# Softmax sums and value products of a window-attention unit on TensorE: issued one after the other, or side by side on alternating tiles

## The chip, the cores and the metric

The kernel runs on one core of one Trainium2 chip. The metric is the device time of one execution in microseconds (us), lower is better. All data are 32-bit floats.

## The reference

The input `x` is an image batch of shape 16 x 56 x 56 x 384 (batch, height, width, channels). Two layers follow each other, each with a residual connection:

```
x = x + attention(groupnorm(x))        # 7x7 windows, shifted by 3, 12 heads of 32
x = x + depthwise3x3(groupnorm(x))     # weights replaced by their signs
```

The attention of a window, per head, over its 49 tokens:

```
score = q @ k.T / sqrt(32) + bias      # 49 x 49, with masks in the last windows
attn  = softmax(score)                 # exp, divided by its sum over the keys
out   = attn @ v                       # 49 x 32
```

The change concerns the last two lines: the sums over the keys, by which the result is divided, and the products with the values.

## The kernel before, in words

**Strips and units.** An image is cut into 8 strips of 7 rows, a strip into 8 windows. The attention works on units of 4 windows, that is half a strip: there are 16 x 8 x 2 = 256 units, numbered `u`. An even `u` is the first half of a strip, an odd one the second.

**The scores come out transposed.** `scores` (line 570) leaves in PSUM, for each head, the keys on the partitions and the queries along the columns. Of the two windows of a pair, one has its keys on partitions 0 to 48, the other on 64 to 112. VectorE scales them and adds the bias (`softmax`, line 587), ScalarE takes the exponential (`exponential`, line 605). The result is the tile `es`, and it is not divided yet.

**Sums and products.** With the keys on partitions, TensorE can do both. `add_up` (line 640) multiplies a matrix of ones, 49 x 32, with the exponentials: each output row holds the sum over the keys, 32 times over, which is what the division needs. There are 8 such matmuls in a unit, one for each of four groups of heads (`i`) and two windows of a pair (`w`), with 294 columns each. `attend` (line 661) multiplies values, 49 x 32, with exponentials, 49 columns at a time: 48 matmuls a unit, over 3 heads of a group (`j`), 2 pairs (`r`), and again `i` and `w`.

**Tiles of TensorE.** Both kinds of matmul use 64 rows and 32 columns of the array at a time, and so one of 8 tiles: `w` chooses the upper or lower rows, `i` the columns. The order of the loops hands the tiles out in turn: `i` and `w` are the innermost loops. A 32-bit matmul of the program stands in the trace as two matmuls, each with a weight load of its own.

**What follows.** `invert` takes the reciprocal of the sums: a logarithm and an exponential on ScalarE (lines 679 and 680), then two operations on VectorE that refine it (lines 681 and 682). The sums lie in the PSUM banks that the scores had used, so the next unit's scores must wait until line 681 has read them. `attend` ends with two copies on ScalarE that bring the products from two PSUM banks (`po`) to SBUF (line 671). `divide` multiplies the two on VectorE (line 689). In an odd unit `project` (line 700) then multiplies the strip's result with the output weights.

**The order of the work.** It is written out by hand and no scheduler changes it. `all_units` goes over the units. Each has a list of six pieces of heavy work, `todo` (the matmuls with 128 x 128 weights and 392 columns: queries and keys at line 503, values at 516, the projection at 700). Sums, inversion, products and division come behind the first piece, the scores of the next unit behind the third (even units) or the fourth (odd units) piece. Between the pieces stands light work of the second layer (`side`), mostly on VectorE. The values reach `attend` through DMAs issued on SyncE's queue; `await_values` puts the wait for them on the first sum of a strip. Four PSUM banks are shared by all other matmuls in turn (`bank`).

Of the kernel before, what the change touches and what calls it, by code (L numbers as in the profile page):

```python
# [34 lines left out]
def kernel(  # L35
# [12 lines left out]
    nc = tc.nc  # L48
# [3 lines left out]
    D = C // NH  # L52
    NC = C // P
    HPC = P // D
    T = WIN * WIN
# [4 lines left out]
    UPS = NW // UW  # L60
    NU = NS * UPS
    HT = 64
# [30 lines left out]
    def bank(name):  # L93
        return ps.tile([P, 512], F32, tag="mm", name=name)
# [6 lines left out]
    ones = const.tile([P, P], F32, tag="ones", name="ones")  # L101
# [385 lines left out]
    raw, sums = {}, {}  # L487
# [12 lines left out]
    def query_key(s, m):  # L500
        pq = bank(f"pq_{s}_{m}")
        for c in range(NC):
            nc.tensor.matmul(  # L503
                pq[:, :ST].rearrange("p (w t) -> p w t", t=T),
                wq_t[:, c, m * P : (m + 1) * P],
                xn[:, c, :, :T],
                start=(c == 0),
                stop=(c == NC - 1),
            )
        nc.scalar.copy(qk[:, m, :ST], pq[:, :ST])  # L510

    def value(s, m):

        pv = bank(f"pv_{s}_{m}")
        for c in range(NC):
            nc.tensor.matmul(  # L516
                pv[:, :ST].rearrange("p (w t) -> p w t", t=T),
                wq_t[:, c, 2 * C + m * P : 2 * C + (m + 1) * P],
                xn[:, c, :, :T],
                start=(c == 0),  # L520
                stop=(c == NC - 1),
            )
        nc.scalar.copy(vt[:, m, :, :T], pv[:, :ST].rearrange("p (w t) -> p w t", t=T))  # L523

    def turn(s, m):

        nc.vector.transpose(  # L527
            vq[:, :, :, m].rearrange("p h n d -> p n h d"),
            vt[:, m].rearrange("p (n w) (j b) -> p n (w j) b", w=2, b=D),
        )  # L530
# [3 lines left out]
    def by_key(s):  # L534

        vs[s] = vpool.tile([P, HPC, NW // 2, NC, D], F32, tag="v", name=f"v_{s}")
        carried[s] = []
        for half in range(4):
            for i in range(HPC):
                move = nc.sync.dma_start(  # L540
                    vs[s][half * D : (half + 1) * D, i].rearrange("k n m d -> k (n m d)"),
                    vq[i * D : (i + 1) * D, half].rearrange("k n m d -> k (n m d)"),
                )
                carried[s].append(move.ins.name)

    def await_values(s, product):

        for name in carried.pop(s) if s else ():
            tc.add_manual_dep(
                product.ins,  # L550
                name,
                mybir.DependencyInfo(mybir.DependencyClass.Sync, mybir.DependencyReason.DATA),
                reason="values by key",
            )

    def scores(u, fast):


        s, n = divmod(u, UPS)
        pp = score_banks  # L560
        rows = T if fast else HT
        for j in range(NC):
            for r in range(2):
                for k in range(2 * HPC):
                    i, w = k % HPC, (k + k // HPC) % 2
                    part = slice(i * D, (i + 1) * D)
                    q0 = (n * UW + 2 * r + w) * T
                    row, col = (w, r) if fast else (r, w)
                    k0 = (2 * j + col) * T
                    nc.tensor.matmul(  # L570
                        pp[row * HT : row * HT + rows, i, k0 : k0 + T],
                        qk[part, NC * fast + j, q0 : q0 + rows],
                        qk[part, NC * (not fast) + j, q0 : q0 + T],
                        start=True,
                        stop=True,
                    )
        raw[u] = pp
# [50 lines left out]
    def by_head(u):  # L628

        flat = es.rearrange("k h w q -> k (h w q)")[:, : NH * 2 * T]  # L630
        return flat.rearrange("k (h r q) -> k h r q", h=NH, r=2)

    def add_up(u):

        flat = es.rearrange("k h w q -> k (h w q)")[:, : NH * 2 * T]
        su = raw[u][:, 0:2, : NC * 2 * T]
        for i in range(HPC):
            for w in range(2):
                keys = slice(w * HT, w * HT + T)
                product = nc.tensor.matmul(  # L640
                    su[i * D : (i + 1) * D, w],
                    ones[keys, :D],
                    flat[keys, i * NC * 2 * T : (i + 1) * NC * 2 * T],
                    start=True,
                    stop=True,
                )
                if u % UPS == 0 and i == 0 and w == 0:
                    await_values(u // UPS, product)
        sums[u] = su

    def attend(u, fast):
        s, n = divmod(u, UPS)
        if n == 0:
            ots[s] = two.tile([P, NC, ST], F32, tag="ot", name=f"ot_{s}")
        po = [bank(f"po_{u}_{w}") for w in range(2)]
        for j in range(NC):
            for r in range(2):
                for i in range(HPC):
                    for w in range(2):
                        keys = slice(w * HT, w * HT + T)  # L660
                        nc.tensor.matmul(  # L661
                            po[w][i * D : (i + 1) * D, (2 * j + r) * T : (2 * j + r + 1) * T],
                            vs[s][keys, i, n * 2 + r, j],
                            by_head(u)[keys, i * NC + j, r] if fast else pts[u, j][keys, 2 * i + r, :],
                            start=True,
                            stop=True,
                        )
        ot = ots[s][:, :, n * UW * T : (n + 1) * UW * T]
        by_window = ot.rearrange("p j (r w q) -> p j r w q", r=2, w=2)
        for w in range(2):  # L670
            nc.scalar.copy(
                by_window[:, :, :, w, :], po[w][:, : NC * 2 * T].rearrange("p (j r q) -> p j r q", j=NC, r=2)
            )

    def invert(u):

        su = sums[u]
        ln, inv = (ptpool.tile([P, 2, NC * 2 * T], F32, tag="pt", name=f"{name}_{u}") for name in ("ln", "inv"))
        nc.scalar.activation(ln, su, AF.Ln, bias=least)
        nc.scalar.activation(inv, ln, AF.Exp, scale=-1.0, accum_out=reach[:, 1, u : u + 1])  # L680
        nc.vector.scalar_tensor_tensor(ln, su, -1.0, inv, ALU.mult, ALU.mult)  # L681
        nc.vector.scalar_tensor_tensor(ln, ln, 2.0, inv, ALU.add, ALU.mult)  # L682
        sums[u] = ln
# [257 lines left out]
    side = {}  # L941
# [72 lines left out]
    def all_units(fast, meanwhile=None):  # L1014
        for m in range(NC):
            value(0, m)
            turn(0, m)
        by_key(0)
        for m in range(2 * NC):
            query_key(0, m)  # L1020
        if meanwhile:
            meanwhile()
        scores(0, fast)
        softmax(0, fast)
        normalize(1)
        exponential(0, fast)
        plan(nc.sync)
        for u in range(B * NU):
            todo = heavy(u)
            light = [(w, f, a) for w, f, a in sorted(side.pop(u, []), key=lambda i: i[0])]  # L1030
            more = u + 1 < B * NU

            then = NC if u % UPS else NC - 1
            for i in range(len(todo)):
                run(todo[i])
                if i == 0:
                    if fast:
                        add_up(u)
                    else:
                        for j in range(NC):  # L1040
                            transpose(u, j)
                    if fast:
                        invert(u)
                    attend(u, fast)
                    if fast:
                        divide(u)
                if i == then and more:
                    scores(u + 1, fast)
                    softmax(u + 1, fast)
                if i == then + 1 and more:  # L1050
                    exponential(u + 1, fast)
                while light and light[0][0] - u <= (i + 1) / len(todo):
                    _, g, a = light.pop(0)
                    g(*a)
            for _, g, a in light:
                g(*a)
        for _, g, a in sorted((i for u in side for i in side[u]), key=lambda i: i[0]):
            g(*a)
        side.clear()


    with tc.manual_schedule():
# [29 lines left out]
        def meanwhile():  # L1092
            load_weights(NC)
            add_bias(True)
            clear_conv()
# [80 lines left out]
```

## Time and profile before

| | us |
|---|---|
| median of 3 runs | 4033.58 (4032.53 to 4033.74) |
| profiled execution | 4033.27 |
| its span, first to last instruction | 4031.5 |
| TensorE busy with matmuls | 3951.1 (98%) |
| VectorE busy | 3493.7 (87%) |
| ScalarE busy | 2228.9 (55%) |
| GpSimd busy | 1871.3 (46%) |
| mean granted TensorE clock | 0.991 of full speed |

Busy time of TensorE is the time in which at least one matmul is under way. Matmuls overlap, above all those on different tiles, so a duration in the trace says how long one lasted, and not what it adds to the time; that is read from when the next ones begin. PEld is the weight loads, which run beside the matmuls. In a row of a line's source view, the three durations are minimum, median and maximum in ns. In the waits the three figures are us in total, the number of times, and the longest.

### The profile page before, as it was taken

Reading aid. Unit: us, or ns where it says so; the run is one execution under the profiler, and the core shown is the slowest. Engines: PE = TensorE matmul, PEld = TensorE weight load, DVE = VectorE, ACT = ScalarE, POOL = GpSimd, SP = SyncE. Lnnn points to the kernel's source line nnn. Section 1 sums busy time; section 2 is a strip of 40 time slices with the busy share of each in tenths; the row PEclk is TensorE's granted clock in tenths of the full one; section 3 lists DMA queues with packets and bytes.
Section 4 is the critical chain, followed back from the end, with each engine's and each line's share of the span. In section 5 each row is a group of like instructions: output and inputs, shape, how many; then the busy total and the mean of one; then the engine's idle time right before and its main releaser. Section 6 shows DMA issues by size and latency. Waiting matters only on the chain.

```text
span 4031.5 us, 144681 instructions
## 1 busy us (share of the span) xinstructions
PE 3951.1 (98%) x63189; PEld 2412.2 (60%) x63189; DVE 3493.7 (87%) x3718; ACT 2228.9 (55%) x4690; POOL 1871.3 (46%) x3168
## 2 busy tenths in 40 slices
PE   7999999999999999999999999999999999999987
PEld 5656555555556555556556556555655656556657
DVE  4546989899898998989899898998989899898897
ACT  3545556556565656556556564656556556565552
POOL 6554545355453554545355454554545455452000
PEclk8999999999999999999999999999999999999998
DMA  4323455554545554555554554554545554553444
GB/s 108 84 67 88 111 114 116 109 120 103 117 116 102 126 111 104 113 113 116 107 122 107 114 115 102 125 112 103 114 112 115 108 123 105 114 117 81 114 103 105
DMA packets 801364, 439.36 MB, mean 109 GB/s; under 512 B 671562, under 2 KB 750777, under 8 KB 800720
## 3 DMA queue, kind: packets, MB, share of 16 engines
q1 hardware_dynamic: 711110, 268.40, 31.1%
q0 software_dynamic: 88320, 161.19, 17.2%
q8 instruction: 498, 8.16, 0.9%
q14 instruction: 146, 1.20, 0.1%
q10 hardware_dynamic: 1290, 0.42, 0.0%
HBM read 170.08 MB, written 158.45 MB: 81 GB/s over the span
## 4 chain that ended last, share of the span: by engine, by line
PE 42%; issue 17%; DVE 15%; POOL 14%; DMA 8%; ACT 2%; SPq 1%; DVEq 0%; POOLq 0%; ACTq 0%
PE pq L503 16%; POOL xl L450 10%; PE pv L516 9%; PE py L700 8%; DVE o L828 6%; PE score_banks L570 3%; DMA xl<-in_x_dram 3%; PE po L661 3%; PE score_banks L640 2%; DVE e L587 2%; DVE xt L467 2%; DMA mvd<-mv 1%; DMA mid<-y 1%; DMA gt<-mvd 1%; DVE ln L682 1%
## 5 line engine op out<-in xcount | busy, mean ns | idle before, releaser
L503 PE MATMUL pq<-xn,wq_t 128*128 128x392 f32 x4608 | 1584.9, 496 | 0.0
L450 POOL DMA_DIRECT2D xl<-in_x_dram x1980 | 1331.8, 723 | 143.3 <-DVE xt L467 93.6
L828 DVE SCALAR_TENSOR_TENSOR o<-hp,dw_t,o 128x1568 f32<-128x1568 f32 x752 | 1378.2, 1833 | 5.4
L503 PEld LDWEIGHTS pq<-xn,wq_t 128*128 128x128 f32 x4608 | 845.4, 188 | 595.5 <-ACT x L482 0.4
L516 PE MATMUL pv<-xn,wq_t 128*128 128x392 f32 x2304 | 815.6, 497 | 13.5 <-DVE y L708 13.5
L700 PE MATMUL py<-ot,wo_t 128*128 128x392 f32 x2304 | 819.1, 501 | 7.4 <-DVE ot L689 6.3
L510 ACT COPY qk<-pq 128x392 f32<-128x392 f32 x768 | 368.4, 483 | 562.9 <-PE pq L503 562.7
L720 POOL COPY y<-y 128x63 f32<-128x63 f32 x128 | 56.5, 442 | 1205.2 <-DVE y L708 1205.1
L700 PEld LDWEIGHTS py<-ot,wo_t 128*128 128x128 f32 x2304 | 425.4, 190 | 312.0 <-DVE ot L689 26.0
L516 PEld LDWEIGHTS pv<-xn,wq_t 128*128 128x128 f32 x2304 | 424.4, 189 | 313.1 <-DVE y L708 15.6
L605 ACT ACTIVATE e<-e 128x1176 f32<-128x1176 f32 x256 | 303.2, 1184 | 500.5 <-DVE e L587 499.5
L681 DVE SCALAR_TENSOR_TENSOR ln<-score_banks,inv 128x588 f32<-128x588 f32 x256 | 195.9, 765 | 323.5 <-ACT inv L680 322.4
L523 ACT COPY vt<-pv 128x392 f32<-128x392 f32 x384 | 188.7, 492 | 359.2 <-PE pv L516 358.4
L570 PEld LDWEIGHTS score_banks<-qk 32*49 32x49 f32 x24576 | 266.4, 118 | 146.8 <-issue 115.8
L587 DVE SCALAR_TENSOR_TENSOR e<-score_banks,bias 128x1176 f32<-128x1176 f32 x256 | 347.1, 1356 | 6.1 <-PE score_banks L570 5.9
L661 PEld LDWEIGHTS po<-e,v 49*32 49x32 f32 x24576 | 311.0, 105 | 50.8 <-issue 0.8
L479 ACT COPY x<-xt 128x196 f32<-128x196 f32 x720 | 225.6, 368 | 176.9 <-DVE xt L467 176.7
L661 PE MATMUL po<-e,v 49*32 49x49 f32 x24576 | 309.7, 212 | 0.0
L570 PE MATMUL score_banks<-qk 32*49 32x49 f32 x24576 | 298.9, 218 | 4.4 <-DVE ln L681 2.9
L527 DVE STREAM_TRANSPOSE vq<-vt 128x512 f32<-128x512 f32 x384 | 265.6, 693 | 8.6 <-ACT vt L523 5.4
L492 ACT ACTIVATE xn<-x,coef 128x392 f32<-128x392 f32 x384 | 247.0, 711 | 6.4 <-DVE coef L381 6.4
L708 DVE TENSOR_TENSOR y<-py,x 128x392 f32<-128x392 f32 x384 | 213.2, 555 | 42.9 <-PE py L700 42.6
(183 smaller groups left out, 3303.7 us busy)
## 6 DMA issues: line engine op xcount, KB each, us to landing
v<-vq SPq DMA_DIRECT2D x2048, 48.0 KB
xb<-mid SPq DMA_DIRECT2D x90, 855.5 KB
out_dram<-o SPq DMA_DIRECT2D x736, 98.0 KB
mid<-y POOLq DMA_DIRECT2D x112, 619.5 KB
xl<-in_x_dram POOLq DMA_DIRECT2D x1260, 52.5 KB
mid<-y POOLq DMA_DIRECT2D x15, 354.0 KB
xl<-in_x_dram POOLq DMA_DIRECT2D x180, 28.0 KB
mid<-y POOLq DMA_DIRECT2D x15, 265.5 KB
```

Of the source, the lines that this page charges most:

```text
L450: nc.gpsimd.dma_start(xz[i * D + lo : i * D + hi, c, k : k + n, :], flat[token : token + n * (hi - lo)].rearrange("(k t) c -> t k c", k=n) ...
L492: nc.scalar.activation(xn[:, c, :, :T], xs[s][:, c, :].rearrange("p (w t) -> p w t", t=T), AF.Identity, bias=coef[:, c, 1:2], scale=coef[: ...
L503: nc.tensor.matmul(pq[:, :ST].rearrange("p (w t) -> p w t", t=T), wq_t[:, c, m * P : (m + 1) * P], xn[:, c, :, :T], start=(c == 0), stop=( ...
L510: nc.scalar.copy(qk[:, m, :ST], pq[:, :ST])
L516: nc.tensor.matmul(pv[:, :ST].rearrange("p (w t) -> p w t", t=T), wq_t[:, c, 2 * C + m * P : 2 * C + (m + 1) * P], xn[:, c, :, :T], start= ...
L527: nc.vector.transpose(vq[:, :, :, m].rearrange("p h n d -> p n h d"), vt[:, m].rearrange("p (n w) (j b) -> p n (w j) b", w=2, b=D),)
L570: nc.tensor.matmul(pp[row * HT : row * HT + rows, i, k0 : k0 + T], qk[part, NC * fast + j, q0 : q0 + rows], qk[part, NC * (not fast) + j, ...
L587: nc.vector.scalar_tensor_tensor(e, pp[:, :, : NC * 2 * T].rearrange("q i (n k) -> q i n k", k=T), QSCALE, bias[:, int(s % NS == NS - 1)]. ...
L605: nc.scalar.activation(flat, flat, AF.Exp, accum_out=reach[:, 0, u : u + 1])
L661: nc.tensor.matmul(po[w][i * D : (i + 1) * D, (2 * j + r) * T : (2 * j + r + 1) * T], vs[s][keys, i, n * 2 + r, j], by_head(u)[keys, i * N ...
L700: nc.tensor.matmul(py[:, :ST], wo_t[:, c, m * P : (m + 1) * P], ots[s][:, c, :], start=(c == 0), stop=(c == NC - 1),)
L828: nc.vector.scalar_tensor_tensor(acc, by_half(hp[:, dy : dy + BR, dx : dx + W]), dw_t[:, c, t : t + 1], acc, ALU.mult, ALU.add)
```

## The change

`add_up` takes a list of tiles and is called twice in a unit from within `attend`. The 8 tiles are split into two sides, those with an even and those with an odd `i + w`, as on a chessboard. First the four sums of one side are issued, then all 24 products of the other side, then the four sums of the other side, then the 24 products of the first. `invert` is issued behind all of these and ahead of the two copies; before, it was issued behind the sums and ahead of the products. On ScalarE the order of logarithm, exponential and copies stays as it was. The number and the sizes of the matmuls stay the same, and the wait for the values' DMAs stays on the first sum.

```diff
-    def add_up(u):
+    def add_up(u, tiles):
 
         flat = es.rearrange("k h w q -> k (h w q)")[:, : NH * 2 * T]
-        su = raw[u][:, 0:2, : NC * 2 * T]
-        for i in range(HPC):
-            for w in range(2):
-                keys = slice(w * HT, w * HT + T)
-                product = nc.tensor.matmul(
...
-                if u % UPS == 0 and i == 0 and w == 0:
-                    await_values(u // UPS, product)
-        sums[u] = su
+        first = u not in sums
+        su = sums.setdefault(u, raw[u][:, 0:2, : NC * 2 * T])
+        for i, w in tiles:
+            keys = slice(w * HT, w * HT + T)
+            product = nc.tensor.matmul(
+                su[i * D : (i + 1) * D, w],
+                ones[keys, :D],
+                flat[keys, i * NC * 2 * T : (i + 1) * NC * 2 * T],
+                start=True,
+                stop=True,
+            )
+            if first and u % UPS == 0:
+                await_values(u // UPS, product)
+            first = False
 
     def attend(u, fast):
...
-        for j in range(NC):
-            for r in range(2):
-                for i in range(HPC):
-                    for w in range(2):
+        tiles = [(i, w) for i in range(HPC) for w in range(2)]
+        sides = [[(i, w) for i, w in tiles if (i + w) % 2 == side] for side in range(2)]
+        for k in range(2):
+            if fast:
+                add_up(u, sides[k])
+            for j in range(NC):
+                for r in range(2):
+                    for i, w in sides[1 - k]:
                         keys = slice(w * HT, w * HT + T)
                         nc.tensor.matmul(
...
+        if fast:
+            invert(u)
         ot = ots[s][:, :, n * UW * T : (n + 1) * UW * T]
...
                 if i == 0:
-                    if fast:
-                        add_up(u)
-                    else:
+                    if not fast:
                         for j in range(NC):
                             transpose(u, j)
-                    if fast:
-                        invert(u)
                     attend(u, fast)
```

`fast` is true in the pass that runs here; the other is a fallback for sums out of range.

## The prediction

> **What bounds the kernel now.** I read the page's first part, then the sources of the two lines that move, then a timeline of one unit, and last that timeline cut at chosen instants, which counts the matmuls begun by then. Page and sources:
>
> ```profile
> PE 3951.1 (98%) x63189; PEld 2412.2 (60%) x63189; DVE 3493.7 (87%) x3718; ACT 2228.9 (55%) x4690; POOL 1871.3 (46%) x3168
> L640 PE MATMUL score_banks<-e,ones x4096: 407/432/696, 75.6 to 3926.1; 49*32 49x294 f32 x196
> L661 PE MATMUL po<-e,v x24576: 200/203/285, 76.6 to 3927.8; 49*32 49x49 f32 x200
> ```
>
> TensorE (PE) is occupied 98%, so what one unit costs it returns 256 times. A product in the program is two matmuls in the trace, a first and a second pass, each with its own weight load (PEld): a unit has 16 sum passes and 96 product passes. Timeline of one unit, PE alone (start, length, count):
>
> ```profile
> 2011.19 0.73 PE L640 MATMUL score_banks<-e,ones 49*32 49x294 f32 x16
> 2011.71 1.14 PE L661 MATMUL po<-e,v 49*32 49x49 f32 x96
> 2012.79 4.22 PE L516 MATMUL pv<-xn,wq_t 128*128 128x392 f32 x12
> ```
>
> Sums, products and hand-over take 2012.79 - 2011.19 = 1.60 us. The same stretch cut at 2011.46, 2011.47, 2011.72, 2011.76, 2011.82, 2011.89, 2011.905, 2012.66:
>
> ```profile
> 2011.19 0.48 PE L640 MATMUL score_banks<-e,ones 49*32 49x294 f32 x8
> 2011.19 0.68 PE L640 MATMUL score_banks<-e,ones 49*32 49x294 f32 x9
> 2011.71 0.21 PE L661 MATMUL po<-e,v 49*32 49x49 f32 x2
> 2011.71 0.25 PE L661 MATMUL po<-e,v 49*32 49x49 f32 x9
> 2011.71 0.29 PE L661 MATMUL po<-e,v 49*32 49x49 f32 x17
> 2011.71 0.29 PE L661 MATMUL po<-e,v 49*32 49x49 f32 x17
> 2011.71 0.39 PE L661 MATMUL po<-e,v 49*32 49x49 f32 x18
> 2011.71 1.14 PE L661 MATMUL po<-e,v 49*32 49x49 f32 x96
> ```
>
> Four things are to be seen. (1) All eight sum tiles run at once: eight first passes are in, and the ninth matmul, the first tile's second pass, comes 0.27 us after the start (2011.47 - 2011.19). (2) The tiles' product passes follow 0.043 us apart: the first tile's first begins at 2011.713, its second at 2011.756, the ninth matmul in the cut at 2011.76. (3) After 17 product passes, none begins for about 0.1 us. (4) From then on 78 passes take 2012.65 - 2011.90 = 0.75 us, 9.6 ns each.
>
> I rest the forecast on (3). Count loads and matmuls as places in the program: 16 sum passes fill 32 places, 17 product passes 34 more; the 18th's matmul is place 68. The matmul 64 places earlier, place 4, is the second pass of the first sum: it began at 2011.465 and lasts 0.407 (the minimum of the sums' row), so it ended at 2011.87. The 18th begins at 2011.90. So I read: **TensorE begins nothing that stands 64 places behind an instruction that has not ended**; then 0.03 us pass. The scores, which hold no long matmul, say the same. Their timeline from 2016.93, cut at 2017.16, 2017.19 and 2017.30:
>
> ```profile
> 2016.93 0.42 PE L570 MATMUL score_banks<-qk 32*49 32x49 f32 x32
> 2016.93 0.42 PE L570 MATMUL score_banks<-qk 32*49 32x49 f32 x32
> 2016.93 0.59 PE L570 MATMUL score_banks<-qk 32*49 32x49 f32 x37
> ```
>
> 32 matmuls with their loads, 64 places, and then a pause until the first matmul, about 0.24 us long here, has ended.
>
> **The change part by part.** It removes and adds no matmul, copy or DMA, and no instruction passes a queue other than its own engine's.
>
> *Sums ahead in two groups of four, products of the other four tiles behind each.* In the first half places 1 to 16 are four sums, 17 to 64 are 24 product passes: 6 on each of four free tiles, 6 x 0.043 = 0.26 us, begun almost at once. So that much does run beside the sums. The 25th can follow when places 1 and 2 have ended (0.43). The 26th's matmul is place 68 and waits for place 4, a second sum pass as before: 0.27 + 0.41 + 0.03 = 0.71 us. The rest, some 24 passes, takes 24 x 9.6 ns = 0.23 us at pace (4), or 0.26 at pace (2) on four tiles; the tile is the nearer bound, as the places are free by then. The half takes 0.94 to 0.97 us. The second half is built alike, and its sums cannot begin earlier, since they stand behind the 24 late products. They come one after another instead of waiting ready, so the last sum starts, and frees its places, some 0.05 us late: four tiles of four instructions at 4.8 ns each (half of 9.6, a pair) are 0.08 against 0.02 for a ready group (eight first passes within 0.05 at the start). Last product pass: 0.97 + 0.97 + 0.05 - 0.04 (its own length) = 1.95, at least 0.94 x 2 - 0.04 = 1.84. Before, the last began 2012.65 - 2011.19 = 1.46 after the first sum. The loss is 0.38 to 0.49 us a unit; I take 0.48, since the tile's pace is a measured one. 256 x 0.48 = **123 us** (97 to 125). Some units (one at 2026.10 shows 1.28 where this shows 1.14) run 0.13 longer now; I leave that as it is.
>
> Covered work that loses its cover: in the old order eight sums shared one wait for a second pass's end, and 17 passes' start lay within it; now two such waits stand in a row, each with four tiles idle behind it.
>
> By the Trainium skill (TensorEngine Tiling (Array Packing), Key Properties) tiles operate independently and can load and multiply in parallel; rows (1) and (2) agree for what is begun, row (3) does not for what comes after. By that rule alone each half would last as long as its sums, and the sum would be the first rival's.
>
> A rule of the same skill speaks against the change (TensorE: Matmul & The Clock Gate, Part 3, The mechanism): matmuls keep program order in start and end, strictly first in, first out. Taken so, it would make the order over tiles worth nothing, and the sum 4033; the cuts at 2011.46 and 2011.47 contradict its start half, as the eighth sum's first pass is in before the first sum's second.
>
> *Inversion moved behind the products.* On ACT (ScalarE) nothing changes places: logarithm L679, exponential L680 and two copies L671 stay in that order. The logarithm's wait grows: the last sum's second pass now begins near 0.97 + 0.05 + 0.27 = 1.29 instead of 0.73 - 0.41 = 0.32, so it ends about 0.97 later from the unit's start, and 0.49 later against the big matmuls behind the products. Queued behind it on ACT are L680, L671 and the evictions of the next matmul groups; on DVE (VectorE) L681, L682 and `divide`. Who waits:
>
> ```profile
> PEld py L700 <- DVE ot L689: 26.0, 31, 3.2
> PEld score_banks L570 <- DVE ln L681: 9.2, 12, 3.0
> PEld score_banks L640 <- ACT x L482: 30.1, 54, 0.6
> ```
>
> The projection is the tight one. In the unit at 2026.10 `divide` ends at 2030.99 and the projection's first load is at 2031.56, so 0.57 us are to spare: 0.49 fits, with 0.08 left for the hand-over. If it does not fit, the price is at most 128 odd units x 0.49 = 63 us. Where waits show already, DVE came late through its own queue, and a later L680 costs nothing there. Against it, the other engines get 123 us more for the same work, so the three rows shown and the smaller ones like them, some 100 us in all, can only shrink through that: a gain between 0 and about 40. I set both at nothing. The scores have 2.5 us between L681's end and their start in the unit shown. The two `po` banks are held 0.5 longer; their next users come two groups (4.22 us) later, and the copies ended at 2014.88, 2.1 after the products: cost 0, up to 0.5 a unit if that cover went. The wait for the values' DMAs stays on the unit's first sum: 0.
>
> **Sum.** 4033.27 us is the profiled execution's time (span 4031.5, 1.8 around it; the median of the three runs is 4033.58, so nothing to correct): 4033 + 123 = 4156.
>
> **The rivals.** (a) *Faster*: the products hide. If places came free when an instruction begins rather than when it ends, the late passes would run on beside the sums; a half would be two sum passes, 0.52 us (2011.71 - 2011.19), and the last product would begin near 1.02: 0.44 less a unit, 113 us, 3920. For it: rows (1), (2). Against: with places freed at the start the 18th pass had come at 2011.76, not 2011.90. Chance 0.09. (b) *Only one of the two waits counts*, the second group's second passes starting early or its products reaching the window with the sums already ended: 0.24 a unit, 61 us, 4095. Against: the second half is built like the first. Chance 0.09. (c) *The inversion's delay is not covered* and is added to the stall: 63 more, 4219; half of it 4187. For it: only 0.08 us are left. Chance 0.15. (d) No change, the sums' wait being filled by chance: 0.02. My forecast, the two stalls alone: 0.65.
>
> **How the numbers follow.** Of the forecast, the lower end is 97 us with 30 regained from waits, 4100; the upper 125 and half of (c) and a little more, 4200. The range 4098 to 4200 leaves out (a), (d), most of (b) that falls lower and the whole of (c). A measurement of this kernel can tell about 0.2%, 8 us, from no change. Faster: (a), 0.09; same: 0.02; slower: 0.89.
>
> **What would show it.** Right: sums and products together take near 2.08 us a unit instead of 1.60; cut counts of product passes stand still twice, at about 25 of 48, for some 0.4 us each, and the pause ends 0.03 us after the end of a group's first second pass; matmul counts are the same. Wrong in the mechanism: product passes that go on past 25 while second sum passes run. Wrong in the surroundings: L700's wait for L689 near 90 us instead of 32, or scores waiting for L681.

## The result, and the profile after

| | before | after |
|---|---|---|
| median, us | 4033.66 (4 runs) | 4125.11 (4 runs, 4121.13 to 4126.48) |
| profiled execution, us | 4033.27 | 4121.13 |
| its span, us | 4031.5 | 4119.3 |
| ratio | | 1.0222, 95% interval 1.0209 to 1.0234 |

The changed kernel is slower by 2.2%, 91 us. The range 4098 to 4200 holds it; the forecast of 4156 was 31 us too high. The page's first row and the two lines' sources, after:

```profile
PE 4055.2 (98%) x63189; PEld 2469.2 (60%) x63189; DVE 3491.2 (85%) x3718; ACT 2230.8 (54%) x4690; POOL 1880.3 (46%) x3168
L640 PE MATMUL score_banks<-e,ones x4096: 404/407/698, 74.2 to 4013.4; 49*32 49x294 f32 x196
L665 PE MATMUL po<-e,v x24576: 200/203/287, 74.4 to 4014.5; 49*32 49x49 f32 x200
```

Counts and durations of single matmuls are what they were; TensorE is busy 104 us longer with the same work. Where they go is seen in the timeline of one unit, TensorE alone (start, length, operation, count; rows in which sums and products follow each other within hundredths of a microsecond are left out):

```profile
2054.33 0.45 PE L640 MATMUL score_banks<-e,ones 49*32 49x294 f32 x4
2054.36 0.42 PE L665 MATMUL po<-e,v 49*32 49x49 f32 x20
2054.60 0.41 PE L640 MATMUL score_banks<-e,ones 49*32 49x294 f32 x1
...
2054.62 0.20 PE L665 MATMUL po<-e,v 49*32 49x49 f32 x2
...
2054.79 0.70 PE L665 MATMUL po<-e,v 49*32 49x49 f32 x22
2055.30 0.41 PE L640 MATMUL score_banks<-e,ones 49*32 49x294 f32 x1
...
2055.54 0.41 PE L640 MATMUL score_banks<-e,ones 49*32 49x294 f32 x1
...
2055.73 0.76 PE L665 MATMUL po<-e,v 49*32 49x49 f32 x24
2056.42 4.22 PE L516 MATMUL pv<-xn,wq_t 128*128 128x392 f32 x12
```

The row at 2054.79 holds the 25th product pass and 21 later ones. When the 26th begins is told by the same timeline cut at 2055.031 and at 2055.043:

```profile
2054.79 0.20 PE L665 MATMUL po<-e,v 49*32 49x49 f32 x1
2054.79 0.45 PE L665 MATMUL po<-e,v 49*32 49x49 f32 x2
```

So 24 product passes begin within 0.3 us beside the sums, as the change wants it. Then only one more pass begins in 0.42 us (2054.62 to 2055.04), while four tiles lie idle and the other four are busy with the sums' second passes. The second pass of the group's first sum runs from 2054.60 for 0.41 us; 0.03 us after its end the products go on. The same happens again after 2055.61: one pass at 2055.73, the next after 2055.54 + 0.41 + 0.03. The unit takes 2056.42 - 2054.33 = 2.09 us, where it took 1.60. The unit shown is no exception: in 241 of the 256 units 25 product passes of the first half had begun when the first sum's second pass ended, in all 256 units 25 of the second half, and the products went on 0.027 us behind that end (median; the trace works out the ends of matmuls and does not observe them). In the kernel before it was 17 passes in 255 units, and the same 0.027 us.

### The profile page after: what moved, and what is told of

It is laid out like the page before. It is cut to its first block, busy times and chain, and to the rows that moved or that the text cites. A ratio compares the mean times of both kernels' runs of the same rounds, so it can differ in the third digit from the quotient of the medians.

```text
span 4119.3 us, 144679 instructions
## 1 busy us (share of the span) xinstructions
PE 4055.2 (98%) x63189; PEld 2469.2 (60%) x63189; DVE 3491.2 (85%) x3718; ACT 2230.8 (54%) x4690; POOL 1880.3 (46%) x3168
## 4 chain that ended last, share of the span: by engine, by line
PE 91%; DVE 3%; issue 2%; POOL 1%; SPq 0%; ACT 0%; DMA 0%; DVEq 0%; ACTq 0%; POOLq 0%
PE pq L503 36%; PE py L706 18%; PE pv L516 18%; PE po L665 8%; PE score_banks L570 6%; PE score_banks L640 3%; DVE o L834 2%; PE pc L871 1%; POOL xl L450 1%; SPq L540 0%; DVE e L587 0%; DVE xt L467 0%; DVE ln L688 0%; DVE ln L687 0%; DVE vq L527 0%
## 5 line engine op out<-in xcount | busy, mean ns | idle before, releaser
L665 PE MATMUL po<-e,v 49*32 49x49 f32 x24576 | 522.7, 208 | 1.6
L665 PEld LDWEIGHTS po<-e,v 49*32 49x32 f32 x24576 | 407.2, 106 | 106.6 <-DVE y L714 6.4
L640 PE MATMUL score_banks<-e,ones 49*32 49x294 f32 x4096 | 367.6, 415 | 12.3 <-ACT e L605 12.3
L685 ACT ACTIVATE ln<-score_banks,least 128x588 f32<-128x588 f32 x256 | 192.5, 752 | 213.3 <-PE score_banks L640 213.3
```

Of the source, the lines that this page charges most:

```text
L640: product = nc.tensor.matmul(su[i * D : (i + 1) * D, w], ones[keys, :D], flat[keys, i * NC * 2 * T : (i + 1) * NC * 2 * T], start=True, st ...
L665: nc.tensor.matmul(po[w][i * D : (i + 1) * D, (2 * j + r) * T : (2 * j + r + 1) * T], vs[s][keys, i, n * 2 + r, j], by_head(u)[keys, i * N ...
```

## Experiments: which part of the change costs

Each run is compared with runs of the kernel before on the same chip; the time of that is named beside it. The edits of the first three are against the changed kernel.

**The exchange of tiles alone (sides_only).**

```diff
-            if fast:
-                add_up(u, sides[k])
+            if fast and k == 0:
+                add_up(u, tiles)
```

> The changed kernel, but all eight sums are issued first as in the kernel before, then the 24 products of one side, then the 24 of the other: products on four tiles at a time, with no second group of sums. The inversion is still issued behind the products, its order on ScalarE is unchanged. Theory: one wait for a second sum pass a unit instead of two; products on four tiles at 0.043 us a pass instead of the order's own pace cost 0.08 us a unit by the same count of places, 20 us: 4035 to 4055. Rival (four tiles are too few for products): the loss stays, 4100 to 4125. Rival (late inversion): its sums end as early as in the kernel before, so 4034.

Measured: 4043.3 against 4034.67, ratio 1.0023 (1.0014 to 1.0033). One unit of it, TensorE alone:

```profile
2013.82 0.73 PE L640 MATMUL score_banks<-e,ones 49*32 49x294 f32 x16
2014.35 1.22 PE L665 MATMUL po<-e,v 49*32 49x49 f32 x96
```

The products on four tiles at a time cost 0.08 us more than in the unit shown of before (1.22 against 1.14), as expected, and 9 us in all; odd units lose only half as much (the last pass begins at 1.631 us, median, against 1.590). The rival that four tiles are too few for them would have kept 65 to 90 us.

**The two groups of sums alone (split_only).** The products keep their old order over all eight tiles.

```diff
-        for k in range(2):
-            if fast:
-                add_up(u, sides[k])
-            for j in range(NC):
-                for r in range(2):
-                    for i, w in sides[1 - k]:
+        for j in range(NC):
+            for r in range(2):
+                if fast and 2 * j + r in (0, NC):
+                    add_up(u, sides[(2 * j + r) // NC])
+                for k in range(1):
+                    for i, w in tiles:
```

> The changed kernel without the exchange of tiles: the sums stay in two groups of four, each ahead of 24 products, but the products keep the order of the kernel before, over all eight tiles in turn. Theory (nothing begins until what stands 64 places ahead has ended): two waits for a second sum pass a unit as in the changed kernel, last product near 1.88 us after the first sum, 0.42 later than in even and 0.29 later than in odd units before: 91 us, 4110 to 4140. Rival (the exchange, that is products on four tiles at a time beside sums, is what costs): products on all eight tiles again, 4035 to 4055.

Measured: 4109.88 against 4033.47, ratio 1.019 (1.0174 to 1.0205). One unit, TensorE alone:

```profile
2047.13 0.45 PE L640 MATMUL score_banks<-e,ones 49*32 49x294 f32 x4
2047.17 0.30 PE L665 MATMUL po<-e,v 49*32 49x49 f32 x8
2047.41 0.43 PE L640 MATMUL score_banks<-e,ones 49*32 49x294 f32 x4
2047.65 0.61 PE L665 MATMUL po<-e,v 49*32 49x49 f32 x37
...
2048.57 0.66 PE L665 MATMUL po<-e,v 49*32 49x49 f32 x38
2049.16 0.60 PE L516 MATMUL pv<-xn,wq_t 128*128 128x392 f32 x1
```

The time lies at the lower end of the theory's 4110 to 4140, far from the rival's 4035 to 4055. The split alone costs 76 of the 91 us, the exchange alone 9. What costs is that a unit now holds two groups of long matmuls.

**Shorter sums (half_sums, half_sums_one).** The changed kernel, but each sum covers the first 147 of its 294 columns.

```diff
-                su[i * D : (i + 1) * D, w],
+                su[i * D : (i + 1) * D, w, : NC * T],
                 ones[keys, :D],
-                flat[keys, i * NC * 2 * T : (i + 1) * NC * 2 * T],
+                flat[keys, i * NC * 2 * T : i * NC * 2 * T + NC * T],
...
```

> The changed kernel, with each sum only 147 columns wide instead of 294; the other half of the columns is not summed, and the inversion reads the first half twice (one more operation on VectorE, line 681 in two pieces). Products, their tiles and their order stay. Theory (a place 64 back must have ended): both passes get 0.123 us shorter, the second pass of a group's first sum ends near 0.44 instead of 0.68 after the group's start, the pause of the products ends 0.25 us earlier in each of the two groups, 0.49 us a unit, 256 units: 125 us less than the changed kernel's 4121, so about 3996; up to 4020 if the 0.13 us that odd units lost in the kernel before come back. Rival (products are slow because only four tiles take them at a time, or because sums next to them slow them): the products stay as they are, 4110 to 4121. Rival (the late inversion costs the time): the inversion is as late against the big matmuls as before, 4110 to 4121.

Measured: 4040.73 against 4034.67, outside the theory's 3996 to 4020 and far from the rivals' 4110 to 4121. One unit, TensorE alone:

```profile
2014.30 0.33 PE L640 MATMUL score_banks<-e,ones 49*32 49x147 f32 x4
...
2014.49 0.73 PE L665 MATMUL po<-e,v 49*32 49x49 f32 x34
...
2015.22 0.75 PE L665 MATMUL po<-e,v 49*32 49x49 f32 x34
2015.90 0.60 PE L516 MATMUL pv<-xn,wq_t 128*128 128x392 f32 x1
```

The last product pass begins 1.467 us after the unit's first load (median), where it is 1.957 in the changed kernel: 0.49 us, the expected amount, with products, tiles and order unchanged. So the pauses do follow the sums' length. But 256 x 0.49 = 125 us became 84. `half_sums` had cut line 681 into two operations, which lengthened the inversion; `half_sums_one` takes that back (the edit is against `half_sums`).

```diff
-        for h in range(2):
-            nc.vector.scalar_tensor_tensor(ln[:, :, h], su[:, :, h], -1.0, inv[:, :, h], ALU.mult, ALU.mult)
         ln, inv = (t.rearrange("p w a q -> p w (a q)") for t in (ln, inv))
+        nc.vector.scalar_tensor_tensor(ln, inv, -1.0, inv, ALU.mult, ALU.mult)
```

> half_sums again, with line 681 in one operation of full width that reads the reciprocal in place of the sums, so that the inversion takes as long as in the changed kernel. Theory: the 0.1 us that the second operation added were what the projection had no room for; without it the 0.49 us a unit come through, 4121 to 4125 less 125: 3995 to 4015. Rival (part of the shorter unit is lost whatever the inversion does, because other engines now bound it): 4035 to 4042, as half_sums.

Measured: 4032.17 against 4033.47. That is a miss for the theory's figure, and the time lies between its range and the rival's: 93 us came through, and 32 did not. Part of the rival holds. The projection's matmuls waiting for `divide`, in `half_sums_one` and then in the changed kernel:

```profile
PE py L709 <- DVE ot L698: 17.9, 28, 3.4
```

```profile
PE py L706 <- DVE ot L695: 4.0, 3, 3.4
```

14 of the 32 us are this row: in 28 odd units VectorE, which has as much to do in less time, comes late with `divide`. Another 8 or 9 are products delayed in single units (the mean of the last product's start lies 0.09 above its median in even units, 0.02 in the changed kernel). The rest was not located.

**The sums behind all products (sums_last).** Against the kernel before, this keeps the sums in one group and makes the inversion late.

```diff
-                    if fast:
-                        add_up(u)
...
         for j in range(NC):
             for r in range(2):
...
+        if fast:
+            add_up(u, tiles)
+            invert(u)
```

> The kernel before, but with the eight sums behind the 48 products instead of ahead of them; the wait for the values sits on the first product. No sum is beside a product of the same unit, and the sums end about 0.93 us later from the unit's start, at the very end of the unit. Theory: TensorE itself loses nothing in the unit (last column of the sums goes in about where the last product's did, 1.5 us after the start); the inversion is 0.93 us later against the big matmuls, 0.5 of it are spare at the projection, so 0.43 x 128 odd units = 55 us at most: 4034 to 4090. Rival (late inversion is what cost the changed kernel its 88 us, at 0.49 us later): with 0.93 it costs at least as much again, 4150 to 4210.

Measured: 4074.75 against 4034.67, ratio 1.01 (1.0083 to 1.0116). The gap by which the projection's first matmul trails the matmul ahead of it, summed over odd units beyond the usual 0.33 us, is 51.6 us here and 11.7 in the kernel before: a difference of 40 us, and the time went up by 40. So a late inversion has a price when it exceeds what the projection can spare, and 0.93 us do. The changed kernel's 0.49 does not: its row above has 4.0 us in 3 units.

## Experiments: what the forecast left out, and a faster order

**The values' transfers (late_move, no_moves).** In the kernel before, the products of odd units are longer than those of even ones: the last pass begins at 1.590 us (median) instead of 1.461. The forecast took these 0.13 us over into the changed kernel. There, even and odd units are equal (1.959 and 1.957). A look at one odd unit of before, TensorE and then SyncE's queue:

```profile
2026.10 0.73 PE L640 MATMUL score_banks<-e,ones 49*32 49x294 f32 x16
2026.62 1.28 PE L661 MATMUL po<-e,v 49*32 49x49 f32 x96
```

```profile
2024.00 11.08 SPq L540 DMA_DIRECT2D v<-vq  x16
```

The transfers that arrange the next strip's values run across the odd unit's products. `late_move` issues them later in the program, against the kernel before:

```diff
-        if more and not half:
-            todo[NC].append((by_key, (s + 1,)))
+        if more and half:
+            todo[1].append((by_key, (s + 1,)))
```

> The kernel before, but the sixteen DMAs that bring the values by key (issued on SyncE's queue in even units, under way while an odd unit's products run) are issued from the second piece of the odd unit on. Theory A (the 0.13 us by which odd units' products are longer in the kernel before come from those transfers): odd units' products shrink to 1.14 us, 128 x 0.13 = 17 us less: 4017. Theory B (they come from elsewhere): 4034, or more if the values then come late.

Measured: 4087.73 against 4034.67. Theory A's 4017 is out; theory B allowed for more where the values come late, and they do, so the run decides nothing between the two. On SyncE's queue the place in the program only decides what stands ahead of the transfers; nothing ties them to TensorE's progress. They fell behind output stores, and the sums of some units waited for them:

```profile
PE score_banks L640 <- DMA out_dram<-o: 23.3, 12, 3.6
PE score_banks L640 <- DMA v<-vq: 10.9, 5, 3.5
```

Its trace tells more. In 57 odd units of it the last product began at 1.46; few of these transfers' packets fell between the first and the last product there (4 on average, against 39 in the other 71 odd units). `no_moves` leaves the transfers out, against the kernel before:

```diff
+        if s > 2:
+            vs[s], carried[s] = vs[s - 1], []
+            return
```

> The kernel before, but from the fourth strip on the sixteen DMAs that bring a strip's values by key (line 540) are not issued; the products then use the third strip's values. TensorE's instructions are the same, and no sum waits for the values any more. Theory A (the 0.13 us by which odd units' products are longer in the kernel before come from those transfers, which are under way at that time in odd units and never in even ones): the last product of odd units begins at 1.46 us as in even units instead of 1.59, 125 odd units x 0.13 = 16 us less: 4012 to 4022. Theory B (they come from elsewhere, such as the light work on other engines): odd units stay at 1.59, 4030 to 4037.

Measured: 4026.23 against 4032.55, ratio 0.9983 (0.9973 to 0.9992). One odd unit:

```profile
2022.22 0.73 PE L643 MATMUL score_banks<-e,ones 49*32 49x294 f32 x16
2022.74 1.14 PE L664 MATMUL po<-e,v 49*32 49x49 f32 x96
```

The median of odd units is 1.460, and 4 of 128 are longer by over 0.05, where 116 were. Within the unit theory A holds exactly. The time lies between the two theories' ranges, since of the 16 us only 6 reach the end; the projection's trailing gaps grew by 7 (19.0 against 11.7), as with the shorter sums. By what means the transfers slow the products was not tried. In the changed kernel they cost nothing in the unit; that its longer pauses hide them is likely, but was not tried.

**Eight products first (eight_first).** If the pause behind the sums comes from places, work that fits should be put where the pause is not. Against the kernel before:

```diff
-                    if fast:
-                        add_up(u)
...
         for j in range(NC):
             for r in range(2):
...
+                if fast and (j, r) == (0, 0):
+                    add_up(u, tiles)
```

The inversion is issued behind the products, as in the changed kernel.

> The kernel before, with the eight products of the first head and pair (16 passes, one on each tile and its second) ahead of the eight sums, the other 40 behind them; the wait for the values sits on the first product. Theory: the first 16 product passes begin in the time in which TensorE now waits for places, the sums begin 0.11 us later than now, 16 product passes fill 32 of the 64 places ahead of the first sum pass that holds them, and of the 80 passes left 16 to 17 begin by 0.70 us, then none until about 0.79 (first second pass of a sum at 0.36 + 0.41 + 0.03); last product near 1.39 instead of 1.46: 0.07 us a unit, 17 us: 4010 to 4022. Rival (order of sums and products on the tiles is worth nothing beyond the stalls of two groups): 4034.

Measured: 4021.3 against 4033.47, ratio 0.9969 (0.9958 to 0.998): the fastest of all that keep the computation, by 12 us. One even unit, TensorE alone, and its products cut at 2033.72, 2033.79 and 2033.82:

```profile
2033.02 0.31 PE L658 MATMUL po<-e,v 49*32 49x49 f32 x15
...
2033.13 0.69 PE L639 MATMUL score_banks<-e,ones 49*32 49x294 f32 x15
2033.62 1.01 PE L658 MATMUL po<-e,v 49*32 49x49 f32 x80
```

```profile
2033.62 0.29 PE L658 MATMUL po<-e,v 49*32 49x49 f32 x17
2033.62 0.29 PE L658 MATMUL po<-e,v 49*32 49x49 f32 x17
2033.62 0.42 PE L658 MATMUL po<-e,v 49*32 49x49 f32 x19
```

The count of 64 foretold how many would begin (17 of the second lot, by 0.70 us after the start at 2033.01) and when the rest would follow (about 0.79). In even units the last pass begins at 1.415 (median) where 1.39 was expected; 1.461 before. In odd units it begins at 1.455 instead of 1.590, twice the 0.07 us that the count foretold. By means the whole gain stands there: 30 even units are delayed, so that their mean is 1.48 against 1.47 before, while that of odd units is 1.47 against 1.59. So the order is faster by 12 us, but how much of that the count of places explains, and how much a smaller loss to the transfers, was not separated.

## Why the prediction was right, point by point

*The limit of 64 places* held wherever it was put to the test: 24 passes and one behind the changed kernel's groups, 17 in `eight_first`, and pauses that end 0.03 us after a first sum's second pass, also where the sums are half as long. That it is the end, and not the beginning, of the instruction 64 places ahead that counts is what rival (a) got wrong. (Its 2011.76 for the 18th pass is too early: by pace (2) the second tile's third pass was ready near 2011.81. The measured 2011.90 speaks against (a) either way.) The count is what the traces show; what in TensorE holds the 64 places they do not tell.

*Two stalls a unit.* Rival (b) is out: both groups pause. The forecast had the last product at 1.95 us; it is at 1.957 to 1.959 (medians). The even units' loss of 0.50 us stands against 0.48 forecast.

*The odd units' 0.13 us* are the term that was mis-sized. "I leave that as it is" was wrong: in the changed kernel they do not show. The odd units lose 1.957 - 1.590 = 0.37, so 128 x 0.13 = 17 us of the 123 do not appear. By means over all units the last product is later by 0.51 in even and 0.38 in odd units, 114 us instead of 123.

*What other engines give back* was set at nothing, between 0 and about 40. From 114 us to the 88 of the profiled executions it is 26. About 15 were waits of values' matmuls for a bank (line 516 for line 708, 15 times some 1.0 us). The wait for a bank is now met within the products, where it is short. The row of before, and the one of after:

```profile
PEld pv L516 <- DVE y L708: 15.6, 15, 1.3
```

```profile
PEld po L665 <- DVE y L714: 6.4, 20, 0.4
```

The projection's trailing gaps, 11.7 us before and 5.2 now, are another 6. The remaining 5 are not located.

*The late inversion.* Rival (c) is out at 0.49 us: the projection's loads wait in each of the 128 odd units, a quarter of a microsecond each, but its matmuls, which those loads run ahead of, hardly do:

```profile
PEld py L706 <- DVE ot L695: 31.7, 128, 3.6
PE py L706 <- DVE ot L695: 4.0, 3, 3.4
```

The forecast's estimate of 0.08 us to spare held for the load alone: the projection's first load began 0.55 us after `divide` ended (median), and now begins 0.05 us after it, as early as it ever does. The matmul had more to spare: it began 0.88 us after `divide`, now 0.36, and where it had to wait it began after 0.05. So some 0.3 us are still left, and `sums_last` shows the price when they are used up. The forecast also read the end of the copies from `po` too late, at 2014.88; the row holds both copies, which ended at 2014.19, so the cover it counted on was longer:

```profile
2013.50 0.69 ACT L671 COPY ot<-po 128x294 f32<-128x294 f32 x2
```

*A rule of the skill.* That tiles operate independently (TensorEngine Tiling (Array Packing), Key Properties) held for what begins; `split_only` and `half_sums` show the limit that lies across all tiles.

## What to carry to other kernels

Before matmuls of unequal length are put on separate tiles, count instructions, loads included, from the first long one to the last short one that is to run beside it: past 64 the short ones waited here for the long one's end, however idle their tiles were. In this kernel the long matmuls belong together, in one group over all tiles; two small groups paid the wait twice. A matmul that stands as two passes counts four places, two of them loads.

## What the runs showed of the hardware that was not expected

Transfers from one on-chip tile to another (packets of 1536 bytes) beside short matmuls lengthened 96 product passes by 0.13 us, in 116 of 128 odd units; without them it was 4 of 128. The transfers of other kinds that run beside even units did not, though they keep the DMA engines busier (a share of 0.74 in the even unit at 2011.19, of 0.30 in the odd one at 2026.10). And a unit made shorter by 0.49 us passed on only three quarters of it (93 of 125 us), with VectorE busy for 87% of the span, as in the kernel before (85% in the changed kernel).
